# Two graph layers in seven-product form: the first product of each group is put by ScalarE into the PSUM bank in which the second accumulates

## The chip, the cores and the metric

The kernel runs on one core of a Trainium2 chip. The metric is the device time of one execution in microseconds, as the median of several runs. The engines are named as in the profile: PE is TensorE (PEld its weight loads), DVE is VectorE, ACT is ScalarE, POOL is GpSimd, SP is SyncE, which here only issues DMAs.

## The reference

There are 64 graphs of 256 nodes with 512 features; all data are float32. Layer 0 applies three graph convolutions and a residual layer norm, layer 1 a linear graph attention and again a residual layer norm:

```python
gcn(x, W, b) = einsum('bnm,bmh->bnh', adj, x @ W) + b
h = relu(gcn(x, W1, b1)); h = relu(gcn(h, W2, b2))
x = layernorm(x + gcn(h, W3, b3))
q, k = split(x @ Wqk, 2, axis=-1); v = x @ Wv
agg = einsum('bij,bjd->bid', adj, k * mask)
w = mask * einsum('bid,bid->bi', q, agg) / sqrt(512)
out = layernorm(x + softmax(w, axis=1)[:, :, None] * v)
```

## The kernel before

**Pairs and products.** Two graphs are worked on at once (a pair, `G = 2`), so there are 32 pairs. Every matrix product is cut into two by two blocks and done with seven block products in place of eight (Strassen's form). Some operands of the seven products are sums or differences of blocks, made beforehand on DVE or POOL; which of the two makes which is the list `ON_DVE` (read by `unit`, lines 61 and 62). `a_sums` makes those of the node features (tile `S`, or in place in `hT` or `xT`), `adj_sums` those of the adjacency matrix (`aS`, `aT`), `t_sums` those of the gather (`T`), and `support` those of its own output (`sup`, names ending in T5 to T7). The name's prefix tells the place: `h1` and `h2` are the outputs of the first and second aggregation, `c1` to `c3` the three supports, `x` the input features, `a` the adjacency matrix.

**A group.** `seven` (line 104) is a generator with seven steps, one product in each, in the order P1, P7, P6, P2, P5, P4, P3. It holds three PSUM banks, `x`, `v` and `y`, out of eight that are handed out in turn (`bank`). P1 is made in `x` and copied out as `t1` by `out` (ACT copies it to a `tmp` buffer in SBUF; where the group has an addend `plus`, DVE adds that instead). P6, P5 and P3 then accumulate in `x` on top of P1, P4 on top of P7 in `v`. P2 has the bank `y` alone, and the first output block is `c11(y, t1)`: a DVE addition of that bank and the SBUF copy. P6 cannot start before `out` has read P1, since both are in the same bank.

**Eleven groups for a pair.** Three `support` (the products with W1, W2, W3; line 290), two `aggregate` (adjacency times the support, line 331, followed by a relu on ACT, `relu`, line 322), one `adj_times` in `back` (the third convolution with its residual, line 367), one `adj_times` for the gather (line 367), and four in `attention` (`inner` with the letters a, b, c, d; line 546), of which `back`, c and d have an addend. The weights of `attention` come through a ring of seven DMA buffers.

**The order of work.** The schedule is written out by hand: nothing reorders instructions afterwards, and each engine works its own instructions in the order in which the program issues them. Each pass of the main loop advances several generators, letter by letter, by a string: F is `front` (supports and aggregations of pair i), S is `sums` (operand sums for pair i + 1), B is `back` of pair i - 1, G and M its gather and `attention`, E (X and Y at the end) the softmax and last norm, `finish`. `START` serves the first pass, `ORDER` the steady ones, `LAST` and `END` the last two. SP's DMA issues stand in the same order.

**In `back`**, after the layer norm statistics (`bn_stats`, line 444, `inv_std`, lines 374 to 378), `apply` writes the normalised rows: ACT makes `xm` (line 460), DVE makes `r` in place (line 462), and DVE transposes follow (line 488). The transposed rows go through DRAM (`via`, lines 492 and 494) and come back as `x1T`, from which `attention` makes `Z` (lines 524 and 527) and POOL makes `I` (line 59).

Of the kernel before, what the change touches and what calls it, by code (L numbers as in the profile page):

```python
# [9 lines left out]
FP = mybir.dt.float32  # L10
# [4 lines left out]
P = 128  # L15
PAIR = 2
G = PAIR
# [3 lines left out]
def gcn_then_graph_attention(ctx: ExitStack, tc: tile.TileContext, xT, xN, adjT, mask, W1, b1, W2, b2, W3, b3,  # L21
                             WqT, WkT, Wv, out):

    nc = tc.nc
    NPAIR = xT.shape[0]
    N, D = 256, 512
    NH, DC = N // P, D // P
    HD = D // 2
# [2 lines left out]
    KEYS = ("T1", "T2", "T3", "T4")  # L31
    SUP = 9
    SBUFS = 6
    TMP = 5
    ON_DVE = ('a5', 'c2T5', 'c2T6', 'c3T6', 'c3T7', 'h13', 'h23', 'h27', 'x3', 'x5')

    const = ctx.enter_context(tc.tile_pool(name="const", bufs=1))
    pool = ctx.enter_context(tc.tile_pool(name="work", bufs=1))
    small = ctx.enter_context(tc.tile_pool(name="small", bufs=2))
    dram = ctx.enter_context(tc.tile_pool(name="dram", bufs=2, space=bass.MemoryType.DRAM))  # L40
    psum = ctx.enter_context(tc.tile_pool(name="psum", bufs=8, space=bass.MemoryType.PSUM))

    E = mybir.EngineType
    ctx.enter_context(tc.manual_schedule(engines={E.PE, E.DVE, E.Activation, E.Pool, E.SP}))

    def bank(shape=(P, G, N)):
        return psum.tile(list(shape), FP, name="ps", tag="ps")

    def tmp():
        return pool.tile([P, D], FP, name="tmp", bufs=TMP)  # L50

    def add(o, a, b):
        nc.vector.tensor_tensor(o, a, b, op=OP.add)  # L53
# [50 lines left out]
    def seven(mm, shape, c11, c12, c21, c22, plus=None):  # L104

        def out(ps, k):
            t = shaped(shape)
            if plus is None:
                nc.scalar.copy(t, ps)  # L109
            else:  # L110
                add(t, ps, plus[k])
            return t

        x = bank(shape)
        mm(1, x, True)
        t1 = out(x, 0)
        yield
        v = bank(shape)
        mm(7, v, True)
        yield  # L120
        mm(6, x, False)
        u = out(x, 1)
        yield
        y = bank(shape)
        mm(2, y, True)
        t7 = out(v, 2)
        c11(y, t1)
        yield
        mm(5, x, False)
        c22(x, t7)  # L130
        yield
        mm(4, v, False)
        c21(v, u)
        yield
        mm(3, x, False)
        c12(x)
        yield
# [22 lines left out]
    ident = const.tile([P, P], FP, name="ident")  # L160
    make_identity(nc, ident)

    def warm(n):

        ps = bank((P, P))
        for _ in range(n):
            nc.tensor.matmul(ps, lhsT=ident, rhs=ident, start=True, stop=True)

    warm(10)
    wl = {}  # L170
    begin, end = load_w(W1, 1, True)
# [5 lines left out]
    for n, b in ((1, b1), (2, b2)):  # L177
        t = const.tile([P, DC], FP, name=f"b{n}")
# [103 lines left out]
    def support(src, w, who, last=None):  # L282

        sup = lambda: pool.tile([P, G, HD], FP, name="sup", tag="sup", bufs=SUP)
        C = {k: sup() for k in (3, 1, 5, 7, 6)}

        def mm(n, ps, first):
            for g in range(G):
                for c in range(2):
                    nc.tensor.matmul(ps[:, g], lhsT=src[n][:, c, g], rhs=w[n][:, c],  # L290
                                     start=(first and g == 0 and c == 0), stop=(g == G - 1 and c == 1),
                                     skip_group_check=True)

        def c21(v, t):
            add(C[5], v, t)
            unit(who + "T7", C[7], C[3], C[5], OP.subtract)
            unit(who + "T6", C[6], C[7], C[1])

        def c12(x):
            C[2], C[4] = sup(), sup()  # L300
            nc.scalar.copy(C[2], x)  # L301
            unit(who + "T5", C[5], C[5], C[1], OP.subtract)
            sub(C[4], x, C[6])
        steps = seven(mm, (P, G, HD), lambda y, t: add(C[3], y, t), c12, c21, lambda v, t: add(C[1], v, t))
        for _ in range(2):
            next(steps)
            yield
        if last is not None:
            last()
        yield from steps  # L310
        return C

    def aggregate(C, aS, b, who):

        hT = [pool.tile([P, 2, G, N], FP, name="hT", tag="act", bufs=2) for _ in range(2)]
        src, first, rest, last = a_sums(blocks(hT), who)
        blk = blocks(hT)

        def relu(i, j, ps=None):
            o = blk(i, j)  # L320
            for c in range(2):
                nc.scalar.activation(o[:, c], (o if ps is None else ps)[:, c], AF.Relu, bias=b[:, 2 - 2 * j + c:3 - 2 * j + c])  # L322

        def block(i, j, a, t):
            add(blk(i, j), a, t)
            relu(i, j)

        def mm(n, ps, first):
            for c in range(2):
                for g in range(G):  # L330
                    nc.tensor.matmul(ps[:, c, g], lhsT=C[n][:, g, c * P:(c + 1) * P], rhs=aS[n][:, g],  # L331
                                     start=(first and c == 0 and g == 0), stop=(c == 1 and g == G - 1),
                                     skip_group_check=True)
        for k, _ in enumerate(seven(mm, (P, 2, G, P), lambda y, t: block(0, 0, y, t), lambda x: relu(0, 1, x),
                                    lambda v, t: block(1, 0, v, t), lambda v, t: block(1, 1, v, t))):
            if k == 5:
                first()
            if k == 6:
                rest()
            yield  # L340
        return src, last
# [21 lines left out]
    def adj_times(aS, mov, c11, c12, c21, c22, plus=None):  # L363

        def mm(n, ps, first):
            for g in range(G):
                nc.tensor.matmul(ps[:, g], lhsT=aS[n][:, g], rhs=mov[n][:, g], start=(first and g == 0),
                                 stop=(g == G - 1), skip_group_check=True)
        yield from seven(mm, (P, G, HD), c11, c12, c21, c22, plus=plus)
# [63 lines left out]
    def back(i, C, aS, x, mask_t, end, put):  # L433
        r = pool.tile([P, G, NH, D], FP, name="r", tag="xT" if end else "r", bufs=1)
        xb = lambda h, j: x[:, :, h, j * HD:(j + 1) * HD]
        rb = lambda h, j: r[:, :, h, j * HD:(j + 1) * HD]
# [3 lines left out]
        def block(o, a, b, h=None):  # L440
            add(o, a, b)
            if h is not None:
                for g in range(G):
                    nc.vector.bn_stats(st[:, h, g], r[:, g, h, :])
                for g in range(G):
                    nc.vector.bn_aggr(mvt[:, h, g], st[:, h, g])
        yield from adj_times(aS, C, lambda y, t: add(rb(0, 1), y, t), lambda x: block(rb(0, 0), x, xb(0, 0), 0),
                             lambda v, t: block(rb(1, 1), v, t, 1), lambda v, t: add(rb(1, 0), v, t),
                             plus=(xb(0, 1), xb(1, 1), xb(1, 0)))

# [49 lines left out]
        gb = lambda h, j: gt[:, h, :, j * HD:(j + 1) * HD]  # L500

        def gather():
            steps = adj_times(aS, xS, lambda y, t: add(gb(0, 0), y, t), lambda x: nc.scalar.copy(gb(0, 1), x),
                              lambda v, t: add(gb(1, 0), v, t), lambda v, t: add(gb(1, 1), v, t))
            for n, _ in enumerate(steps):
                if n == 6:
                    put["gt"] = gt
                    if i + 2 < NPAIR:
                        aTs[i + 2] = load_adj(i + 2)
                yield  # L510
# [4 lines left out]
    def attention(i, x1b, w, r, mask_t, put):  # L515
# [23 lines left out]
        def inner(q, R, more=None):  # L539

            outer = OUTER[q]

            def mm(n, ps, first):
                wt = ring.pop(at[0])
                for k, o in enumerate(outer):
                    nc.tensor.matmul(ps[:, k], lhsT=left[n](place[o]), rhs=wt[:, k], start=(first and k == 0),  # L546
                                     stop=(k == len(outer) - 1), skip_group_check=True)
                fetch(at[0] + RING)
                at[0] += 1
            if more is None:  # L550
                c12, plus = lambda x: nc.scalar.copy(R[:, :, 0, 1], x), None
            else:
                c12 = lambda x: add(R[:, :, 0, 1], x, more[:, :, 0, 1])
                plus = (more[:, :, 0, 0], more[:, :, 1, 0], more[:, :, 1, 1])
            return seven(mm, (P, len(outer), HD), lambda y, t: add(R[:, :, 0, 0], y, t), c12,
                         lambda v, t: add(R[:, :, 1, 0], v, t), lambda v, t: add(R[:, :, 1, 1], v, t), plus=plus)
        v = pool.tile([P, G, NH, D], FP, name="v", tag="v", bufs=1)
        flat = lambda R: R.rearrange("p g j f -> p g (j f)")
# [35 lines left out]
    def finish(i, prev, gs=range(G)):  # L594
# [22 lines left out]
        for k, g in enumerate(gs):  # L617
            for h in range(NH):
# [2 lines left out]
                yield  # L621
            nc.sync.dma_start(out[i, :, g * NH * D:(g + 1) * NH * D].rearrange("p (h f) -> p h f", h=NH), v[:, g])

    ORDER = ("BBFEFFBEBFBFBFBFFFBEFFFFBFSFBBBFFFBBBFGFFGGFFGFEEGMFFGMMMEGMMSFFMEMMEMMEFESMMEEFFMSM"
             "SMMMFMMMMFFEMMMMMMMMSMMMMMMFSMMMSSMMSSM")
    START = ("FFFBFBBFFBFBBBBBFFFFFFBBBBBFBBBBBBBBBBBFFBBBBSBFFBSBFBBFFFBBFBBFBFSFBFFBBBBFBBSFFBSB"
             "BSFBSFFSBBBSBBBBBSFBBBBBSBSBB")
    LAST = ("FBBSEFBFEBBFFBFBFBFFBFFFFEBBFFBBFBFBEFEEGFEGGFFEGEFFMMGSFFGMMMMFEFMMMMEMMMMMMEMMMFMM"
            "GSMMMMEMMMMMMMMFMMMSSMMMFMSSSFMFFSFSFSM")
    END = ("BEBBBBBBEBBBBBBBBGMGMEMMBEGGEEMGEGEMMMMMMEMEEMEMMMMMMMMMMMGMMBMMMMMMMMMMXMMXXMMMXYXM"  # L630
           "XMYXYMYYMYXYMYXYBMYMMXXYYXM")

    def run(order, rest, **gens):
        res = {}
# [81 lines left out]
```

## Time and profile before

| What | Value |
|---|---|
| time, median of 3 runs | 2762.32 us (2762.25 to 2767.2) |
| the profiled execution's own time | 2765.32 us |
| its span, first to last instruction | 2763.5 us |
| granted TensorE clock in it | 0.996 |
| PE busy | 2716.9 us, 98% |
| PEld busy | 2401.7 us, 87% |
| DVE busy | 2145.0 us, 78% |
| ACT busy | 1133.1 us, 41% |
| POOL busy | 1262.8 us, 46% |
| DMA engines busy, mean | 46.9% |

The float32 matmul of the program is recorded as two MATMUL rows with two LDWEIGHTS rows; counts of rows are therefore twice the counts of instructions. A MATMUL row's duration overlaps the next row's, so the pace of PE is read from start to start, not from the durations. A wait is listed as "engine line waited for": who sat idle, and who ended it.

### The profile page before, as it was taken

How to read it: one execution, taken by the hardware profiler on the slowest of the kernel's cores; microseconds unless marked ns; L12 is line 12 of the kernel's file. 1: busy time of each engine (PE TensorE's matmuls, PEld its weight loads, DVE VectorE, ACT ScalarE, POOL GpSimd, SP SyncE). 2: the span in 40 equal slices, each digit the busy share in tenths (PEclk: the TensorE clock that was granted, in tenths of full speed). 3: DMA queues.
4: the chain of work that ended last, by engine and by line, in shares of the span. 5: the costliest groups of instructions: out<-in, count | busy, mean ns of one | idle time of the engine just before them, and what ended most of it. 6: DMA issues, size and time to landing. Idle time of an engine off the chain costs nothing. (4 is left out here: it accounts for less than half of the span.)

```text
span 2763.5 us, 41007 instructions
## 1 busy us (share of the span) xinstructions
PE 2716.9 (98%) x14290; PEld 2401.7 (87%) x14290; DVE 2145.0 (78%) x3828; ACT 1133.1 (41%) x2050; POOL 1262.8 (46%) x966
## 2 busy tenths in 40 slices
PE   9999999999999999999999999999999999999996
PEld 8888888888888888888888888888888888888885
DVE  5778777877777777778777777877787877778777
ACT  3434344434344343443334443434433444434343
POOL 3535455444554354544445543445544455434442
PEclk9999999999999999999999999999999999999998
DMA  6534554344544445543455444455434554434553
GB/s 209 165 110 147 165 175 135 117 143 154 163 151 123 126 147 162 173 135 112 143 162 162 141 129 131 147 162 176 133 115 141 161 162 148 130 123 147 162 155 97
DMA packets 202233, 403.71 MB, mean 146 GB/s; under 512 B 24752, under 2 KB 61872, under 8 KB 193968
## 3 DMA queue, kind: packets, MB, share of 16 engines
q1 hardware_dynamic: 202032, 401.10, 46.5%
q8 instruction: 117, 1.92, 0.3%
q14 instruction: 84, 0.69, 0.1%
HBM read 328.54 MB, written 72.48 MB: 145 GB/s over the span
## 5 line engine op out<-in xcount | busy, mean ns | idle before, releaser
L109 ACT COPY tmp<-ps 128x512 f32<-128x512 f32 x768 | 431.3, 584 | 643.3 <-PE ps L290 257.1
L62 POOL TENSOR_TENSOR sup<-sup 128x512 f32<-128x512 f32 x160 | 218.1, 1372 | 565.9 <-DVE sup L53 409.2
L546 PE MATMUL ps<-ring,I 128*128 128x256 f32 x1792 | 433.0, 381 | 7.7 <-DVE tmp L53 3.0
L546 PEld LDWEIGHTS ps<-ring,I 128*128 128x128 f32 x1792 | 334.1, 190 | 66.3 <-DVE R L53 11.7
L290 PE MATMUL ps<-w_T,S 128*128 128x256 f32 x1536 | 351.0, 381 | 9.2 <-POOL S L62 7.6
L301 ACT COPY sup<-ps 128x512 f32<-128x512 f32 x96 | 56.2, 586 | 722.2 <-PE ps L290 722.2
L290 PEld LDWEIGHTS ps<-w_T,S 128*128 128x128 f32 x1536 | 286.7, 190 | 59.7 <-POOL S L62 20.5
L546 PE MATMUL ps<-ring,Z 128*128 128x256 f32 x1344 | 327.9, 380 | 1.1 <-ACT Z L524 1.1
L59 POOL TENSOR_TENSOR I<-Z 128x384 f32<-128x384 f32 (+1 forms) x128 | 190.1, 1504 | 244.5 <-DVE Z L527 150.8
L546 PEld LDWEIGHTS ps<-ring,Z 128*128 128x128 f32 x1344 | 254.4, 190 | 38.4 <-ACT Z L524 3.3
L331 PEld LDWEIGHTS ps<-aT,sup 128*128 128x128 f32 x2048 | 253.5, 192 | 13.2 <-issue 6.6
L331 PE MATMUL ps<-aT,sup 128*128 128x128 f32 x2048 | 261.8, 276 | 1.8
L53 DVE TENSOR_TENSOR R<-ps,tmp 128x512 f32<-128x512 f32 (+1 forms) x384 | 221.2, 616 | 48.7 <-PE ps L546 48.4
L62 POOL TENSOR_TENSOR x<-x,b3b 128x512 f32<-128x512 f32 x128 | 192.2, 1523 | 128.7 <-DMA x<-in_xN 119.3
L290 PE MATMUL ps<-w,hT 128*128 128x256 f32 x1024 | 242.0, 379 | 0.0
L290 PE MATMUL ps<-w_T,hT 128*128 128x256 f32 x1024 | 236.5, 379 | 0.0
L290 PEld LDWEIGHTS ps<-w_T,hT 128*128 128x128 f32 x1024 | 194.6, 190 | 26.5
L53 DVE TENSOR_TENSOR sup<-ps,tmp 128x512 f32<-128x512 f32 x288 | 192.8, 677 | 30.8 <-PE ps L290 30.7
L290 PEld LDWEIGHTS ps<-w,hT 128*128 128x128 f32 x1024 | 192.0, 190 | 24.7
L331 PE MATMUL ps<-aS,sup 128*128 128x128 f32 x1536 | 206.3, 279 | 1.7 <-ACT tmp L109 1.1
L322 ACT ACTIVATE hT<-hT,b 128x256 f32<-128x256 f32 x384 | 167.4, 501 | 87.1 <-DVE hT L53 86.2
L331 PEld LDWEIGHTS ps<-aS,sup 128*128 128x128 f32 x1536 | 188.9, 192 | 11.4 <-DVE hT L53 4.8
(116 smaller groups left out, 4762.8 us busy)
## 6 DMA issues: line engine op xcount, KB each, us to landing
ring<-mv SPq DMA_DIRECT2D x672, 256.0 KB, 3.6
x<-in_xN SPq DMA_DIRECT2D x32, 1024.0 KB, 8.0
out<-v SPq DMA_DIRECT2D x64, 512.0 KB, 7.6
xT<-in_xT SPq DMA_DIRECT2D x31, 1024.0 KB, 5.0
via<-tr SPq DMA_DIRECT2D x31, 1024.0 KB, 4.2
x1T<-via SPq DMA_DIRECT2D x124, 256.0 KB, 4.7
ring<-mv SPq DMA_DIRECT2D x224, 128.0 KB, 3.1
aT<-in_adjT SPq DMA_DIRECT2D x32, 512.0 KB, 3.9
```

The source lines that it names most:

```text
L53: nc.vector.tensor_tensor(o, a, b, op=OP.add)
L59: (nc.gpsimd).tensor_tensor(o, a, b, op=op)
L62: (nc.vector if name in ON_DVE else nc.gpsimd).tensor_tensor(o, a, b, op=op)
L109: nc.scalar.copy(t, ps)
L290: nc.tensor.matmul(ps[:, g], lhsT=src[n][:, c, g], rhs=w[n][:, c], start=(first and g == 0 and c == 0), stop=(g == G - 1 and c == 1), skip ...
L301: nc.scalar.copy(C[2], x)
L322: nc.scalar.activation(o[:, c], (o if ps is None else ps)[:, c], AF.Relu, bias=b[:, 2 - 2 * j + c:3 - 2 * j + c])
L331: nc.tensor.matmul(ps[:, c, g], lhsT=C[n][:, g, c * P:(c + 1) * P], rhs=aS[n][:, g], start=(first and c == 0 and g == 0), stop=(c == 1 and ...
L546: nc.tensor.matmul(ps[:, k], lhsT=left[n](place[o]), rhs=wt[:, k], start=(first and k == 0), stop=(k == len(outer) - 1), skip_group_check= ...
```

## The change

A group gets its bank `y` from a tag of its own with two banks (`seed_bank`); the eight banks become six and two. Once P1 is in `x`, ACT copies it into `y`, a copy from PSUM to PSUM (with an addend, DVE adds it on the way). P2 is then issued without the start flag, so that it accumulates on top of P1 in `y`. The callback `c11` gets the finished block: it is an ACT copy or, in `aggregate`, the relu straight from PSUM, where before it was a DVE addition. Two banks are first written by matmuls, eight in all, at the start of the program. The list `ON_DVE` is another one: new on it are a3, a6, a7, c1T6, c1T7, c2T7, h17, h25 and h26; c2T5, c3T6 and h13 have left it, to POOL. The four order strings are other ones.

```diff
     TMP = 5
-    ON_DVE = ('a5', 'c2T5', 'c2T6', 'c3T6', 'c3T7', 'h13', 'h23', 'h27', 'x3', 'x5')
+    SEEDS = 2
+    ON_DVE = ('a3', 'a5', 'a6', 'a7', 'c1T6', 'c1T7', 'c2T6', 'c2T7', 'c3T7', 'h17', 'h23', 'h25', 'h26', 'h27', 'x3', 'x5')
...
-    psum = ctx.enter_context(tc.tile_pool(name="psum", bufs=8, space=bass.MemoryType.PSUM))
+    psum = ctx.enter_context(tc.tile_pool(name="psum", bufs=8 - SEEDS, space=bass.MemoryType.PSUM))
...
+    def seed_bank(shape=(P, G, N)):
+        return psum.tile(list(shape), FP, name="seed", tag="seed", bufs=SEEDS)
...
         x = bank(shape)
         mm(1, x, True)
-        t1 = out(x, 0)
+        y = seed_bank(shape)
+        if plus is None:
+            nc.scalar.copy(y, x)
+        else:
+            add(y, x, plus[0])
         yield
...
-        y = bank(shape)
-        mm(2, y, True)
+        mm(2, y, False)
         t7 = out(v, 2)
-        c11(y, t1)
+        c11(y)
...
+    seeds = [seed_bank((P, 4, P)) for _ in range(SEEDS)]
+    for t in seeds:
+        for k in range(4):
+            nc.tensor.matmul(t[:, k], lhsT=ident, rhs=ident, start=(k == 0), stop=(k == 3), skip_group_check=True)
     warm(10)
...
-        steps = seven(mm, (P, G, HD), lambda y, t: add(C[3], y, t), c12, c21, lambda v, t: add(C[1], v, t))
+        steps = seven(mm, (P, G, HD), lambda y: nc.scalar.copy(C[3], y), c12, c21, lambda v, t: add(C[1], v, t))
...
-        for k, _ in enumerate(seven(mm, (P, 2, G, P), lambda y, t: block(0, 0, y, t), lambda x: relu(0, 1, x),
+        for k, _ in enumerate(seven(mm, (P, 2, G, P), lambda y: relu(0, 0, y), lambda x: relu(0, 1, x),
...
-            return seven(mm, (P, len(outer), HD), lambda y, t: add(R[:, :, 0, 0], y, t), c12,
+            return seven(mm, (P, len(outer), HD), lambda y: nc.scalar.copy(R[:, :, 0, 0], y), c12,
...
-    ORDER = ("BBFEFFBEBFBFBFBFFFBEFFFFBFSFBBBFFFBBBFGFFGGFFGFEEGMFFGMMMEGMMSFFMEMMEMMEFESMMEEFFMSM"
-             "SMMMFMMMMFFEMMMMMMMMSMMMMMMFSMMMSSMMSSM")
+    ORDER = ("BBFEFFBEFBBFBFBFFBFFFFFBBBFBBBFFGSFFFGEGFGGFFGEFMMGMEMFEFMFMEMFMMEMFMSMFMSEMSEESMMF"
+             "SSMFFMMMSEMMFSFMMMMMMMMSMMMMMEMMMMMSMMF")
...
```

The two `adj_times` calls change as the `inner` line does; `START`, `LAST` and `END` change as `ORDER` does.

More of the change, by code (lines that the diff above doesn't have):

```diff
@@ L446, in block @@
                     nc.vector.bn_aggr(mvt[:, h, g], st[:, h, g])
-        yield from adj_times(aS, C, lambda y, t: add(rb(0, 1), y, t), lambda x: block(rb(0, 0), x, xb(0, 0), 0),
+        yield from adj_times(aS, C, lambda y: nc.scalar.copy(rb(0, 1), y), lambda x: block(rb(0, 0), x, xb(0, 0), 0),
                              lambda v, t: block(rb(1, 1), v, t, 1), lambda v, t: add(rb(1, 0), v, t),
@@ L502, in gather @@
         def gather():
-            steps = adj_times(aS, xS, lambda y, t: add(gb(0, 0), y, t), lambda x: nc.scalar.copy(gb(0, 1), x),
+            steps = adj_times(aS, xS, lambda y: nc.scalar.copy(gb(0, 0), y), lambda x: nc.scalar.copy(gb(0, 1), x),
                               lambda v, t: add(gb(1, 0), v, t), lambda v, t: add(gb(1, 1), v, t))
@@ L622, in finish @@
             nc.sync.dma_start(out[i, :, g * NH * D:(g + 1) * NH * D].rearrange("p (h f) -> p h f", h=NH), v[:, g])
-    ORDER = ("BBFEFFBEBFBFBFBFFFBEFFFFBFSFBBBFFFBBBFGFFGGFFGFEEGMFFGMMMEGMMSFFMEMMEMMEFESMMEEFFMSM"
-             "SMMMFMMMMFFEMMMMMMMMSMMMMMMFSMMMSSMMSSM")
[L626 to L631, printed above, removed]
+    ORDER = ("BBFEFFBBEFBBFBFBFFBFFFFFBBBFBBBFFGSFFFGEGFGGFFGEFMMGMEMFEFMFMEMFMMEMFMSMFMSEMSEESMMF"
+             "SSMFFMMMSEMMFSFMMMMMMMMSMMMMMEMMMMMSMMF")
+    START = ("BBBFFFFFBFFBBBBBFFFFFFFBBBBFBBBFBSBBBBBBSBBBBBBFBFSBFBBFFBFBFFFBBBBFBFBBBFBFBSFFBBBS"
+             "BBSFSBBBBFBBBFBSBBSBSSFSBBBBB")
+    LAST = ("FFBEFBBBEBBFFBFBFFBFFFFSFBSFFFBBBFBBFFEGEFEGGFGFFGMMGFMFGMEMFFMEMMMMMMMMMFFMMEMEEFEF"
+            "MSFSMFEMSSMMMFMMSMMMMMMSMMMMESFMMMMSSMM")
+    END = ("BBEBBBBBEBBBBBBBBGBGMEGEGMEMEMMGMEEGMMMEMMEMMMEEMMMMMGMMMBMMMMBMMMMMMMMMMXMMXMXMMXYX"
+           "MMXYYMXXYYXYYMXYYXYYMMYXMMM")
     def run(order, rest, **gens):
```

## The prediction, made before the changed kernel was run

> **What bounds the kernel now.** First the page: the busy times and the slices.
>
> ```profile
> PE 2716.9 (98%) x14290; PEld 2401.7 (87%) x14290; DVE 2145.0 (78%) x3828; ACT 1133.1 (41%) x2050; POOL 1262.8 (46%) x966
> ...
> PE   9999999999999999999999999999999999999996
> PEclk9999999999999999999999999999999999999998
> ```
>
> PE is busy in every slice at the full clock, except in the last. Busy is not yet at its pace, so I turned to the timeline. In the stretch 1096:1122, eight MATMUL rows of 256 columns start at 1098.33 and the next row at 1100.06: 0.216 us a row. Eight of 128 columns start at 1107.83, the next at 1108.72: 0.112. The groups by shape hold 10,304 rows of 256 columns and 3,712 of 128, some 270 small ones besides: 10,304 x 0.216 + 3,712 x 0.112 + about 31 = 2,672 us. The first matmul starts at 1.4, the last ends 9.3 before the span's end. So of 2763.5 about **80 to 84 us** are gaps between matmuls: 8 in the first 86 us, 21 in the last 100, and in between (by start-to-start distance above the pace) 1.2 to 2.8 in each stretch of 86, about **1.75 us for a pair**. That is all that the other four engines can give back in the steady part; the rest is PE's own pace.
>
> Where are these gaps? The waits of PE and PEld name two kinds that can be traced to one place each:
>
> ```profile
> PEld ps L290 <- POOL S L62: 20.5, 32, 0.8
> PEld ps L546 <- DVE R L53: 12.4, 30, 0.9
> PE ps L290 <- POOL S L62: 7.6, 32, 0.4
> PEld ps L546 <- DVE tmp L53: 7.1, 11, 1.0
> ```
>
> (us in total, times, longest.) The first comes once for each pair, and the timeline shows it with the end of the first aggregation:
>
> ```profile
> 1111.76 1.86 PEld L331 LDWEIGHTS ps<-aT,sup 128*128 128x128 f32 x16 [0.22 <-issue]
> 1112.10 0.67 DVE L53 TENSOR_TENSOR hT<-ps,tmp 128x512 f32<-128x512 f32 x1
> 1112.87 2.62 ACT L322 ACTIVATE hT<-hT,b 128x256 f32<-128x256 f32 x6 [0.74 <-DVE hT L53]
> 1113.02 1.52 DVE L53 TENSOR_TENSOR hT<-ps,tmp 128x512 f32<-128x512 f32 x2 [0.25 <-PE ps L331]
> 1113.77 1.16 PE L331 MATMUL ps<-aS,sup 128*128 128x128 f32 x8
> 1114.77 1.89 PE L290 MATMUL ps<-w,hT 128*128 128x256 f32 x8
> 1115.56 1.27 POOL L62 TENSOR_TENSOR S<-hT 128x512 f32<-128x512 f32 x1 [5.11 <-ACT hT L322]
> 1116.89 3.72 PE L290 MATMUL ps<-w_T,S 128*128 128x256 f32 x16 [0.23 <-POOL S L62]
> ```
>
> P1 of the second support (1114.77, eight rows) would be over at 1116.50; P7 starts at 1116.89, when POOL has made h17. That is **0.39 us**, and it recurs: 31 times, 12.3 us in all. The other gaps of this stretch are a P5 that waits for ACT's copy of P6 (0.22), starts after a wait (0.07 to 0.12 each) and a P3 that waits for DVE (0.12). The second kind lies in the c and d products of line 546, where P5 and P3 wait for DVE's copy or sum of the same bank: up to 0.77 us in one pair, none in another, about 11 us in all.
>
> **What the Trainium skill says.** "PSUM — Partial Sum Buffer", The four PSUM rules: writes by ScalarE or VectorE leave the has_written bits alone, and a matmul without the first flag adds to what an engine has written where the bit is set. That is what the eight first matmuls are for, so the change can do what it says; the trace of before holds no such write. "Perfetto Trace Analysis", Optimizing Scalar/DVE Operations: a ScalarE operation has about 51 ns of access overhead on PSUM and 93 on SBUF. The trace has no copy into PSUM; the nearest row is ACT tmp<-ps, 584 ns. The same section says that GpSimd and DVE share an SBUF port. The trace agrees: S<-hT on DVE (h27) takes 984 ns where POOL works beside it, S<-hT,S 671; sums of POOL go from 1.27 to 1.5 us.
>
> **The change part by part.** The order of the built program, engine by engine, was laid beside before's.
>
> 1. *DVE and ACT.* Each group loses one DVE addition: 352, of which 320 at 0.68 and 32 at 0.415 us by their rows, 231 us of 2145. ACT gains a copy in nine of eleven groups (288; 256 at 0.585 and 32 of half the size): about 160 us. The SBUF copy of P1 becomes the PSUM copy, and the relu reads PSUM in place of SBUF (463 for 501 ns). Neither engine is the bound, so this by itself is worth **0**; its cover is PE, with 98%.
>
> 2. *The new dependence.* P2 waits for the copy into y. But P6 comes before P2 in each group and always waited for the same reading of P1, since it accumulates in that bank. In the built order no P2 waits for a copy. So the chain P1, copy, P6 is the one to price. In the first aggregation P6 follows P1 by one product of 0.90 us; the copy starts 0.2 after P1 and takes 0.58, and about 0.1 goes to the start: 0.88. Before, the same place cost 0.09 and 0.07. By the nearest row: **0**. Bounds: 0.04 less by the skill's overheads, which gives at most 1 us over 31 pairs; 0.2 more, if copies within PSUM were slower, some 6 us loss. In all other groups P6 starts 1.7 us or more after P1, which covers even that.
>
> 3. *Banks.* Two for y, six for x and v. A third group's copy waits for the c11 of the group two earlier; ACT and the program have it in that order anyway, and P2 of that group is long issued. Six banks that turn in twos come round after three groups, eight that turn in threes after 2.67. **0**; cover: the order itself, in which each bank's last reader stands well over 1 us before the next start.
>
> 4. *h17 to DVE.* POOL was idle for 5.1 us before it, so no queue held it; its own 1.27 us did. On DVE, with POOL idle beside it, 0.68: the chain is 0.6 shorter, the gap was 0.39. It stands in DVE's order right behind the addition that feeds the relu, and DVE waits there for ACT (0.9 us) with nothing urgent behind it but row transposes. **-0.39 x 31 = -12 us**. Bounds: 0 (if relu is later by what item 6 says) and -15 (with the slow start of P6 behind it).
>
> 5. *c and d.* DVE loses both c11 additions that stood in its order between the sums for P5 and P3. In the new order P5's sum is done 0.7 us before PE comes to it, and P3's 0.85 (by rows of 0.6 and 0.41 us from start to start); in the old one P3 had 0.25. **-10 us** of the 11, bounds 0 and -13. The ring of SP is the new limit there: the new order has up to 20 M steps with no F between them, 14 before. Landing is 3.6 us median, seven buffers ahead are at least 4.3; three waits of 0.5 to 0.7 were seen. Up to +5 us.
>
> 6. *The apply on ACT.* In the new order the first `apply` (0.80 us; 0.74 from start to start) stands before the copies of P6 and P7 of the first aggregation; before, it came after four relus. It waits for DVE's norm scale. DVE works without a pause for 11 us before: four v updates of 0.66, three additions to r, four statistics of 0.6, five sums of sup, and the small ones of the scale among them. Added up from the softmax column, the scale is there 0.5 us before P6 ends, so the copy is late by 0.2 and P5 by 0.2, about the 0.22 that P5 already waits. **0**, bounds -3 and +30 (below).
>
> 7. *Other units.* a3, a6, a7, c1T6, c1T7, c2T7, h25, h26 go to DVE, c2T5, c3T6, h13 to POOL: with h17 192 more on DVE net. By the rows (three of 0.42, six of 0.7, less three of 0.7) that is 107 us, which leaves DVE some 124 below before; POOL loses about 210 (rows of 0.7 to 1.4). c1T6 and c1T7 feed the first aggregation's P6 and P7; DVE has them 0.2 to 0.6 us before. h13 is ready 1.4 us before its P3. **0**, for the cover of item 5's DVE slack; bounds +-5.
>
> 8. *SP.* 1,275 DMAs as before, and the via store stands between the same ring loads. The last transpose ends where it did (0.2 us apart by the same sums), so Z comes when it came. **0**, +-2.
>
> 9. *Start and end.* Eight cold matmuls: 16 rows at 0.223 (warm(10) takes 4.46 us for 20) = 3.6 us, of which P7's 1.74 and P6's 0.39 us of waiting for weights and S take up 2.1: **+1.5**. The end keeps its chain of scores, softmax and norm: 0, +-2.
>
> Sum: -12 - 10 + 1.5 = -20.5. Because items 4 to 7 all stand on slacks under a microsecond, of which some will be used up, I take 2.5 back: **-18 us**. Against the profiled execution, 2765.3 (span 2763.5 and 1.8 around it), that is 2747.3; the median of the runs shown is 3.0 below that execution, so 2744.3, put at **2744**.
>
> **Rivals.** *(A) Small gain*, as above: 2728 to 2756, chance 0.64. *(B) Nothing*: P7's gap turns into waits of P5 and P3 behind the apply, and c and d are held by the ring: -12 - 10 + 1.5 + 31 x 0.65 = 0, 2762, within 0.2%. For it speaks that the timeline has five short gaps one behind another there; against it, that DVE loses work. Chance 0.14. *(C) Slower*: DVE's 16 longer operations before the scale take their full rows, not their distances: 16 x 0.08 = 1.3 us later. Then P7 of the first aggregation waits for c1T7 and P5 behind the apply, together 1.2 more in each pair: +37, less 10 of c and d and item 4's gain lost, +1.5: +28, 2790. It decides from where the scale is over 0.8 us later than summed. The rows measured back to back in the old stretch speak against it. Chance 0.22. That the bank would not accumulate is excluded by the eight matmuls; it would not change the time.
>
> **Numbers.** Range 2730 to 2774: A and B whole, and C's nearer part. A measurement of this kernel tells about 0.2%, 5.5 us, from no change. Faster 0.64, within 0.14, slower 0.22. A's own range is 2728 to 2756.
>
> **What would show it.** PE's rows and pace the same, gaps down to about 1.1 us for a pair; L290's wait for S at P7 gone, L546's waits for DVE under 3 us; DVE near 2020, ACT near 1300, POOL near 1050. Wrong if PE waits for ACT at line 342 (the aggregation's line in the changed kernel) by over 0.5 us in each pair, or for the ring.

## The result and the profile after

The changed kernel takes **2786.79 us** (median of 6 runs, 2783.62 to 2788.93) against 2764.03 for the kernel before (6 runs beside it): a ratio of **1.008, 95% interval 1.0067 to 1.0093**. It is 23 us slower; 18 us faster was forecast, with a range of 2730 to 2774. The profiled execution took 2786.89 us, with a span of 2785.1 at a granted clock of 0.995.

(In the diff under "The change" one letter is missing: the new `ORDER` begins `BBFEFFBBEFBBFBFBFFBFFFFFBBBF`.)

The page after, the same rows as before:

```profile
PE 2711.8 (97%) x14306; PEld 2410.4 (87%) x14306; DVE 2146.5 (77%) x3668; ACT 1276.8 (46%) x2338; POOL 1102.6 (40%) x774
...
PE   9999999999999999999999999999999999999996
...
PEclk9999999999999999999999999999999999999997
```

Clock and pace are as before, PE still fills every slice. DVE has lost 160 instructions and yet is as busy as before (2020 was forecast). The waits of PE and PEld (us in total, times, longest):

```profile
PE ps L342 <- ACT tmp L113: 27.0, 31, 0.9
PE ps L557 <- ACT Z L535: 13.7, 26, 1.4
```

```profile
PEld ps L342 <- issue: 32.0, 31, 1.0
PEld ps L557 <- ACT Z L535: 27.1, 35, 1.8
```

The waits for `S` and for `R` that led the list before are gone from its head. Two others stand there, and both were priced at nothing: PE waits for ScalarE at line 342, the aggregation, once for each pair, which the prediction had named as its sign of error; and PE waits for Z.

The timeline at the end of the first aggregation shows the first (start, us, engine, line, operation):

```profile
1116.98 1.68 POOL L66 TENSOR_TENSOR sup<-sup 128x512 f32<-128x512 f32 x1 [23.26 <-DVE sup L66]
...
1117.39 0.57 ACT L122 COPY seed<-ps 128x512 f32<-128x512 f32 x1 [0.36 <-PE ps L342]
1117.65 1.02 DVE L389 SCALAR_TENSOR_TENSOR nb<-mvt,rs 128x4 f32<-128x4 f32 x1
1118.61 0.68 DVE L60 TENSOR_TENSOR sup<-ps,sup 128x512 f32<-128x512 f32 x1
...
1119.01 1.06 PE L342 MATMUL seed<-aT,sup 128*128 128x128 f32 x8
...
1119.27 0.15 DVE L467 SCALAR_TENSOR_TENSOR mnb<-nb,mask 128x4 f32<-128x4 f32 x1
1119.51 0.81 ACT L471 ACTIVATE xm<-r,mnb,mrs 128x512 f32<-128x512 f32 x1 [1.55 <-DVE mnb L467]
1120.23 1.05 ACT L113 COPY tmp<-ps 128x512 f32<-128x512 f32 x2
...
1120.93 1.24 PE L342 MATMUL ps<-aT,sup 128*128 128x128 f32 x9 [0.87 <-ACT tmp L113]
```

Read it from the bottom. P5 (1120.93) waits for ScalarE's copy of P6. P6 was issued to its last row when P2 began, at 1119.01, so the copy could have run 0.2 us later; it starts at 1120.23, because the first `apply` stands in front of it on ScalarE. That `apply` waited for the scale, `mnb`. And the scale is late by one operation: `nb`, four elements in each of 128 partitions, takes **1.02** us. In the kernel before it took 0.16:

```profile
1111.42 0.16 DVE L378 SCALAR_TENSOR_TENSOR nb<-mvt,rs 128x4 f32<-128x4 f32 x1
```

POOL's sum c1T5 runs from 1116.98 to 1118.66, and `nb` ends when it ends. That is so in 31 pairs: each time `nb` ends 0.02 us after the sum.

To see where the time went I sorted PE's gaps (start to start, less the pace of 0.216 and 0.112 us) by the product that was late, for every profiled kernel. "Ends" are the first 86 and the last 110 us; the other columns are the 30 odd pairs between. P7 is that of the second support, which needs h17; P6 is the next product there; P5 that of the first aggregation (all its gaps between aT products); I are the products of line 557 with sums of Z.

| kernel | time | P7 | P6 | P5 | Z | I | P3s and other | ends | all gaps |
|---|---|---|---|---|---|---|---|---|---|
| before | 2764.0 | 12.3 | 3.2 | 9.0 | 2.1 | 13.7 | 13.2 | 30.1 | 83.6 |
| changed | 2786.8 | 0.0 | 0.0 | 34.3 | 22.6 | 5.3 | 10.1 | 31.2 | 103.5 |
| seeding, old order | 2806.0 | 12.1 | 3.2 | 9.0 | 1.0 | 53.7 | 13.0 | 28.1 | 120.1 |
| before + h17 on DVE | 2784.3 | 0.0 | 13.7 | 9.0 | 4.5 | 10.3 | 35.0 | 27.4 | 100.1 |
| before, seven banks | 2801.5 | 12.2 | 3.2 | 9.0 | 1.7 | 50.6 | 13.2 | 30.7 | 120.8 |
| changed + c1T5 on DVE | 2755.4 | 0.0 | 0.0 | 24.9 | 0.0 | 3.9 | 10.3 | 28.9 | 68.0 |
| changed + early scale | 2766.2 | 0.0 | 0.0 | 17.7 | 21.1 | 4.6 | 10.0 | 31.3 | 84.6 |
| changed + both | **2732.6** | 0.0 | 0.0 | 1.4 | 0.0 | 4.6 | 10.3 | 31.9 | 48.3 |
| both, h17 on POOL | 2748.0 | 12.1 | 3.2 | 1.4 | 0.3 | 6.4 | 9.8 | 31.4 | 64.6 |

The second row less the first: P7 and P6 give 15.5 back, I 8.4, the rest 2; P5 takes 25.3 and Z 20.5. That is +19.9 of the 21.6 by which the span grew.

### The profile page after: what moved, and what is told of

It is laid out like the page before. It is cut to its first block, busy times and chain, and to the rows that moved or that the text cites. A ratio compares the mean times of both kernels' runs of the same rounds, so it can differ in the third digit from the quotient of the medians.

```text
span 2785.1 us, 41190 instructions
## 1 busy us (share of the span) xinstructions
PE 2711.8 (97%) x14306; PEld 2410.4 (87%) x14306; DVE 2146.5 (77%) x3668; ACT 1276.8 (46%) x2338; POOL 1102.6 (40%) x774
## 5 line engine op out<-in xcount | busy, mean ns | idle before, releaser
L113 ACT COPY tmp<-ps 128x512 f32<-128x512 f32 x512 | 280.2, 586 | 205.2 <-PE ps L301 114.3
L557 PE MATMUL ps<-ring,Z 128*128 128x256 f32 x896 | 226.2, 384 | 13.8 <-ACT Z L535 13.7
L57 DVE TENSOR_TENSOR sup<-ps,tmp 128x512 f32<-128x512 f32 x192 | 130.5, 680 | 136.3 <-PE ps L301 136.3
L342 PEld LDWEIGHTS ps<-aT,sup 128*128 128x128 f32 x1536 | 193.7, 192 | 38.4 <-issue 32.0
L342 PE MATMUL ps<-aT,sup 128*128 128x128 f32 x1536 | 199.5, 277 | 27.0 <-ACT tmp L113 27.0
L122 ACT COPY seed<-ps 128x512 f32<-128x512 f32 x256 | 146.8, 574 | 161.9 <-PE ps L301 120.5
L557 PEld LDWEIGHTS ps<-ring,Z 128*128 128x128 f32 x896 | 164.8, 190 | 47.4 <-ACT Z L535 27.1
L301 PE MATMUL ps<-w,S 128*128 128x256 f32 x768 | 181.6, 380 | 3.0 <-DVE sup L57 3.0
L566 ACT COPY R<-seed 128x512 f32<-128x512 f32 (+1 forms) x128 | 67.0, 549 | 242.0 <-PE seed L557 219.1
L57 DVE TENSOR_TENSOR R<-ps,tmp 128x512 f32<-128x512 f32 (+1 forms) x256 | 149.2, 617 | 25.8 <-PE ps L557 24.9
```

The costliest lines, as they stand in the source:

```text
L122: nc.scalar.copy(y, x)
L566: return seven(mm, (P, len(outer), HD), lambda y: nc.scalar.copy(R[:, :, 0, 0], y), c12, lambda v, t: add(R[:, :, 1, 0], v, t), lambda v, ...
```

## The experiments

Two explanations stood against each other at first. **Theory (port):** POOL's sum holds the small DVE operation that makes the scale, and everything behind it follows. **Rivals:** the seeding costs by itself (copies into PSUM, six banks); or DVE's order is simply too full, and `nb` is only where that shows.

### Seeding with the old order

```
 (the changed kernel, with these of the kernel before)
 ON_DVE = ('a5', 'c2T5', 'c2T6', 'c3T6', 'c3T7', 'h13', 'h23', 'h27', 'x3', 'x5')
 ORDER, START, LAST, END
```

> The seven-product groups of the changed kernel (P1 written into the bank of P2, two banks kept), with the order of steps and the units on VectorE of the kernel before. Theory (port): the loss of the change comes from the new order and not from the seeding. Without it the scale of the norm comes long before it is wanted, so P5 of the first aggregation waits no more than 0.3 us; P7 still waits 0.39 us for h17, c and d lose 4 to 10 us of their waits (fewer sums on VectorE), and the start costs 1.5: 2752 to 2762 us. Rival (seeding costs): the copies into PSUM and the two banks hold PE whatever the order: 2775 us or more, with P6 or P5 waiting for ScalarE by 0.5 us or more in each pair.

Measured: 2806.05 us, ratio 1.0151 (1.0137 to 1.0165). Both expectations failed. The time is what the rival gave, but not by its wait: P5 waits 0.22 as before, P6 no more than before. The 40 us stand at one product, the first of c and d with I, 1.4 us in each pair. The timeline there:

```profile
1147.34 3.62 POOL L63 TENSOR_TENSOR I<-Z 128x512 f32<-128x512 f32 x2 [8.39 <-DVE Z L538]
1148.88 1.03 PE L557 MATMUL ps<-ring,Z 128*128 128x256 f32 x4
1150.36 0.68 DVE L57 TENSOR_TENSOR gt<-ps,tmp 128x512 f32<-128x512 f32 x1
1151.04 1.28 POOL L63 TENSOR_TENSOR I<-I,Z 128x512 f32<-128x512 f32 x1
1151.14 1.10 PE L557 MATMUL ps<-ring,I 128*128 128x256 f32 x4 [1.23 <-POOL I L63]
```

The profile names POOL. But the first of the two I sums, the one that this product reads, ended at 1149.3, and the kernel before had the same sums at the same distance without a wait. What ends 0.1 us before the start is DVE's `gt<-ps`, at 1151.04: the sum that reads a bank of the gather. In 30 pairs the weight load of this product starts 0.070 to 0.071 us after the end of that sum, while its distance to POOL's second sum varies from 0.138 to 0.146. This points to the bank: of six, it comes round one reader too early. The next run tests that.

### Seven banks, nothing seeded

```
-psum = ... tc.tile_pool(name="psum", bufs=8, ...)
+psum = ... tc.tile_pool(name="psum", bufs=7, ...)
```

> The kernel before with seven PSUM banks in place of eight, nothing seeded. Theory (banks): in the old order of steps the banks are used to the last one; the first products of c and d of line 546 come to wait for the gather's and the aggregation's sums on VectorE, as they do in the run that seeds with the old order (where the wait is 1.4 us at c's P7): 1 to 2.5 us in each pair, 2790 to 2840. Rival (eight banks had slack, and the wait in that run is GpSimd's sum I, which the profile names): within 0.3% of before.

Measured: 2801.52 us, ratio 1.0127 (1.0112 to 1.0143), as the theory gave. The I column rises by 37, the whole of the loss, and no other moves. The old order of steps has no bank to spare. The list of waits names nobody for it ("issue"), but the timeline shows whom the first of these products waits for. Of the two sums in the first line, the one that ends first does so at 1152.85:

```profile
1152.17 1.27 DVE L53 TENSOR_TENSOR hT<-ps,tmp 128x512 f32<-128x512 f32 x2
1152.92 0.73 PEld L546 LDWEIGHTS ps<-ring,I 128*128 128x128 f32 x4 [1.02 <-issue]
```

In 30 pairs the load starts 0.07 us after the end of that `hT` sum, which reads a bank too; these waits make 24 us.

So a kernel that keeps two banks for seeds needs another order of steps, and the changed kernel's has it: its I column is 5.3. The counterpart, the new order without seeds, was not run, so what the seeding alone is worth stays open.

### h17 alone

```
-ON_DVE = (..., 'h13', 'h23', ...)        (kernel before)
+ON_DVE = (..., 'h13', 'h17', 'h23', ...)
```

> The kernel before with one edit: h17 on VectorE in place of GpSimd. Expected by the prediction's item 4: the 0.39 us that P7 waits in each pair goes, and nothing else moves: 31 x 0.39 = 12 us less, 2752 us. Rival: VectorE's sum stands in front of the additions that PE wants next (P3, P5 of the weights' product), or comes no sooner since VectorE is behind: 2760 to 2766, with a new wait for VectorE there.

Measured: 2784.32 us, ratio 1.0073 (1.006 to 1.0085); the rival's kind of loss, larger than it gave. P7's gap is gone. The timeline shows what came for it:

```profile
1121.41 0.69 DVE L62 TENSOR_TENSOR S<-hT 128x512 f32<-128x512 f32 x1 [0.97 <-ACT hT L322]
...
1122.09 0.15 DVE L456 SCALAR_TENSOR_TENSOR mnb<-nb,mask 128x4 f32<-128x4 f32 x1
...
1122.33 0.81 ACT L460 ACTIVATE xm<-r,mnb,mrs 128x512 f32<-128x512 f32 x1 [0.95 <-issue]
```

In the old order `mrs` and `mnb` stand behind h17, and h17 waits for ScalarE's last relu. The first `apply` starts 1.67 us after P1 of the second support (1120.66), before it was 0.62. P6 then waits for a copy behind the apply, and P3 of the same support for a DVE sum behind the normalized rows and their transposes: 10.5 and 21.8 us. The edit pays only where nothing that the chain needs is queued behind h17.

### c1T5 on DVE, the scale early, and both

```
 ON_DVE: + 'c1T5'                            (first)
 back:   rs, nb = inv_std(mvt)
-        yield                               (second)
         mrs = ...; mnb = ...
+        yield
```

> The changed kernel with one more unit on VectorE: c1T5 leaves GpSimd, so that no GpSimd sum runs beside the small operation nb that makes the norm's scale. Theory (port): nb falls from about 0.97 to 0.2 us; but c1T5 now takes 0.68 us of VectorE ahead of the scale, so that the scale comes only 0.1 to 0.3 us sooner and P5 still waits some 0.8 us: 2775 to 2787. Rival (VectorE's order is too full, nb is only where it shows): nb stays long or the scale comes 0.6 us later, P5 waits 1.5 us or more: 2795 to 2810.

> The changed kernel with mrs and mnb right behind nb (the half of the run with both edits that leaves c1T5 on GpSimd). Theory (port): nb is still held to about 0.97 us by GpSimd's sum, but the first apply starts some 0.55 us sooner than in the changed kernel, since one addition less stands between nb and mnb; P5's wait falls from 1.03 to some 0.5 us, Z's waits shrink by about two thirds: 2757 to 2768, between the run with c1T5 alone on VectorE and the changed kernel. Rival (only VectorE's own queue matters, GpSimd's sum does no harm): as fast as the run with both edits, 2730 to 2740, with nb at 0.2.

> The changed kernel with c1T5 on VectorE and with the two operations mrs and mnb, which make the scale, right behind the norm's nb instead of one step later. Theory (port): the scale is there 0.8 us or more sooner, the first apply ends before ScalarE's copies of P6 and P7 are due, P5's wait falls from 1.03 to 0.1 us or less, and Z comes about 1 us sooner, so that its waits (11 us) shrink too: 2745 to 2758. Rival (the seeding or the full VectorE holds PE): P5 waits, or other waits take over, 2775 or more.

Measured, with the ratio to before:

| | c1T5 on POOL | c1T5 on DVE |
|---|---|---|
| scale one step later | 2786.79, 1.008 (changed kernel) | 2755.37, 0.997 (0.9959 to 0.9982) |
| scale right behind nb | 2766.21, 1.0002 (0.9994 to 1.001) | **2732.59, 0.9886 (0.9872 to 0.9899)** |

Taking c1T5 from POOL gives 31 to 34 us, the early scale 21 to 23, and they add up. With both, in the same stretch:

```profile
1097.46 0.16 DVE L389 SCALAR_TENSOR_TENSOR nb<-mvt,rs 128x4 f32<-128x4 f32 x1
...
1097.66 0.16 DVE L466 SCALAR_TENSOR_TENSOR mnb<-nb,mask 128x4 f32<-128x4 f32 x1
1097.74 0.68 DVE L66 TENSOR_TENSOR sup<-sup 128x512 f32<-128x512 f32 x1
1097.90 0.81 ACT L471 ACTIVATE xm<-r,mnb,mrs 128x512 f32<-128x512 f32 x1
...
1099.01 1.07 ACT L113 COPY tmp<-ps 128x512 f32<-128x512 f32 x2 [0.29 <-PE ps L342]
...
1099.70 1.55 PE L342 MATMUL ps<-aT,sup 128*128 128x128 f32 x12
```

`nb` is back at 0.16, the apply is over before P6 is (P2 begins at 1098.81), and P5 follows P2 after eight rows of 0.112. DVE has 32 operations of 0.69 more here than in the changed kernel, so a DVE that is too full is ruled out. Seeding and six banks are the same in all four, and the fastest is 32 us below the kernel before, so they do not make the 23 us by themselves. The rival of the early scale, that POOL's sum does no harm, gave 2730 to 2740; it fell too, with `nb` still at 1.02 and P5's wait at 0.50.

Two details of the expectations failed: the early scale was to shrink Z's waits by two thirds and left 21.1 of 22.6, and c1T5 on DVE came 20 us below its range, all of it at Z. (Both edits together came 12 us below theirs.) So Z isn't late because of the scale. It has a hold of its own. Of the four normalizing operations of a pair (`r<-r,rs,nb`, line 473) the second stands behind h17 in DVE's order, whenever the scale was there. In the changed kernel:

```profile
1125.37 1.62 DVE L473 TENSOR_SCALAR r<-r,rs,nb 128x512 f32<-128x512 f32 x1
1125.43 1.27 POOL L66 TENSOR_TENSOR S<-hT,S 128x512 f32<-128x512 f32 x1 [6.77 <-DVE S L66]
```

and with c1T5 on DVE:

```profile
1109.49 0.55 DVE L473 TENSOR_SCALAR r<-r,rs,nb 128x512 f32<-128x512 f32 x1
1109.62 1.56 POOL L66 TENSOR_TENSOR S<-hT,S 128x512 f32<-128x512 f32 x1 [32.27 <-DVE S L66]
```

POOL's h16 starts 0.06 us behind the operation in one and is let through first; in the other it starts 0.13 us behind and is the one that waits. From P1 of the second support (medians over 24 pairs) the last transpose ends and the first copy of Z ends:

| kernel | last transpose | first copy of Z | PE at its first Z |
|---|---|---|---|
| before | 8.94 | 21.17 | 22.23 |
| changed | 7.02 | 19.74 | 19.92 |
| changed + early scale | 7.02 | 19.81 | 19.92 |
| changed + c1T5 on DVE | 5.96 | 19.12 | 19.92 |
| both | 5.96 | 19.12 | 19.92 |

The hold moves the end of the transposes by 1.06 us, the early scale by nothing. It isn't new: in the kernel before the same operation took 1.64 us in 30 pairs. But the slack of 1.06 us that Z had there (22.23 less 21.17) is 0.18 in the changed kernel. Why POOL's start shifts by 0.07 us isn't settled; it had stood idle for 32.27 us there, against 6.77.

The medians hide something. Z's waits aren't spread evenly: 17.8 of the 22.6 us stand in 10 of 30 pairs. In just these ten the store of the transposed rows, `via`, landed 5.6 to 6.2 us after its issue, in the other twenty after 4.2 to 4.3. And in each of the ten a DMA of 16 KB from another queue (q8, which the page lists as "instruction") began 0.9 to 2.2 us after the issue of the store, in none of the twenty. Of the stretches 1044.9:1051.2 (first two lines) and 1130.9:1137.2 (the third):

```profile
q8 instruction: 1, 0.02, 1.7%
via<-tr SPq DMA_DIRECT2D x1, 1024.0 KB, 6.1
...
via<-tr SPq DMA_DIRECT2D x1, 1024.0 KB, 4.3
```

With the early scale it is the same (11 pairs, 17.1 of 21.1 us). In the two kernels with c1T5 on DVE such a DMA comes 3.9 us after the issue at the earliest, and the store never takes over 4.8. So c1T5 on DVE brings two things at once: the transposes end 1.06 us sooner, and no q8 transfer begins early in the store. Which of them frees Z the runs don't separate; the second was planned by nobody, and is luck. That the small DMA delays the store is read from the coincidence, not tested.

### The apply behind the copies

```
-ORDER = "BBFEFFBBEFBBFBFBFFBFFFFFBBBF...
+ORDER = "BBFEFFBBEFBBFBFBFFFFFBFFBBBF...     (changed kernel)
```

> The changed kernel with the step that holds the first apply put behind P6, P2 and the copies of P6 and P7 of the first aggregation in the order string (two steps of the front between). Theory: P5's wait of 1.03 us at the first aggregation goes (to 0.1 or less), which proves that the apply in front of the copies made it; but the apply itself starts later beside PE's work by 1.5 us or so, and Z, which had no slack left, is late by as much more: its waits grow from 22 to 50 us or more, so that the time is 2790 to 2815. Rival (the apply's place alone costs, Z has slack): 2752 to 2760.

Measured: 2820.35 us, ratio 1.0194 (1.018 to 1.0208). P5's gap falls to the level of small starts (4.4 for all pairs), so the apply in front of the copies did make it. But the loss isn't at Z (15.1, less than in the changed kernel); it is at P3 of the same aggregation, whose gap grows by 61 us:

```profile
1137.10 0.83 ACT L471 ACTIVATE xm<-r,mnb,mrs 128x512 f32<-128x512 f32 x1
1137.96 0.55 DVE L473 TENSOR_SCALAR r<-r,rs,nb 128x512 f32<-128x512 f32 x1 [2.33 <-ACT xm L471]
1138.55 1.03 DVE L499 STREAM_TRANSPOSE tr<-r 128x256 f32<-128x256 f32 x2
1139.44 1.25 DVE L57 TENSOR_TENSOR hT<-ps,tmp 128x512 f32<-128x512 f32 x2
1140.15 1.05 PE L342 MATMUL ps<-aS,sup 128*128 128x128 f32 x7 [1.99 <-DVE hT L57]
```

The step moves DVE's part too. DVE stands idle for 2.33 us before the normalizing operation, and the sum `hT`, which PE needs for P3, waits behind it. That chain was in no expectation; a step moved for ScalarE's sake moves every engine's queue. Another 10 us come from PE itself: behind the wait, in 7 pairs, some rows of 256 columns start 0.427 us apart instead of 0.216. The next run shows more of that.

### h16 on DVE

```
 ON_DVE: + 'h16'                              (changed kernel)
```

> The changed kernel with one more unit on VectorE: h16, the sum that GpSimd begins 0.06 us after VectorE's second normalizing operation (r<-r,rs,nb, line 473) and during which that operation takes 1.62 in place of 0.55 us. Theory (Z is late in part for this): the second operation falls to 0.55, h16 itself takes 0.68 of VectorE ahead of it, so that the last transpose ends some 0.4 us sooner; Z's waits fall from 22 to about 10 us, P5's wait stays at 1.03: 2772 to 2780. Rival (Z is late only since the scale is late, the held operation has slack): 2785 or more, up to 2806 with 0.68 more on VectorE.

Measured: 2926.2 us, ratio 1.0582 (1.0567 to 1.0596), far from both. h16 doesn't stand ahead of the held operation in DVE's order; between h17 and h16 stand three normalizing operations and six transposes:

```profile
1179.45 1.62 DVE L473 TENSOR_SCALAR r<-r,rs,nb 128x512 f32<-128x512 f32 x1
1179.52 1.27 POOL L66 TENSOR_TENSOR hT<-hT 128x512 f32<-128x512 f32 x1 [6.78 <-DVE S L66]
...
1184.83 0.66 DVE L66 TENSOR_TENSOR S<-hT,S 128x512 f32<-128x512 f32 x1
...
1185.64 3.44 PE L301 MATMUL ps<-w_T,S 128*128 128x256 f32 x8 [3.15 <-DVE S L66]
1188.91 1.89 PE L301 MATMUL seed<-w,hT 128*128 128x256 f32 x8
```

PE waits 3.15 us for it, and then its eight rows take 3.44 us where the next eight take 1.89. In the stretch right behind the wait the granted clock, the third number from the right, is 0.50:

```profile
1185.60:1188.00 2.40, 2.36 (x6) 1.94 (x7) 0.48 (x1) 0.00 (x0) 1.76 (x2) 0.50 0.89 333
```

It is so in 29 of 30 pairs, for 5 to 13 rows. Of the 139 us over the changed kernel the waits make 99 and the rows at half the pace 48; Z's 22 go, since PE comes later. And the operation is held as before: POOL's next sum has taken h16's place beside it. So this run doesn't test what it was meant to.

### h17 back on POOL

```
 ON_DVE: - 'h17'                              (the kernel with both edits)
```

> The kernel with both edits (c1T5 on VectorE, mrs and mnb early), but with h17 back on GpSimd, which undoes the prediction's item 4 where nothing else holds PE. Theory: P7 of the second support waits again for GpSimd's h17, 0.39 us in each pair, and h16 behind it comes later: 2742 to 2750, against 2732.6. Rival (in the new order GpSimd's h17 comes in time): 2730 to 2735.

Measured: 2748.04 us, ratio 0.9944 (0.993 to 0.9957), inside the theory's range. The gap of 0.39 is back at P7 (12.1) and the slow start at P6 behind it (3.2): 15.3 together, and the times differ by 15.5.

```profile
PEld ps L301 <- POOL S L66: 20.3, 32, 0.8
```

### The port by itself

```
for f in forms:              # one form of DVE operation at a time
    8 x nc.gpsimd.tensor_tensor(c, a, b, op=add)     # 128x512, in SBUF
    10 x f()                 # e.g. scalar_tensor_tensor(n, s, -1.0, u), 128x4
```

> VectorE's operations by themselves, ten of each form one behind another, first beside eight sums of GpSimd (128x512, all in SBUF), then with GpSimd idle; none of the reference is computed. Theory (port): small operations with two SBUF sources (the form of nb, and an addition of 128x4) take 0.15 us with GpSimd idle and wait for the end of a running GpSimd sum beside it, so that one of them takes about as long as a GpSimd sum (1 us or more); those with one SBUF source, or one of PSUM and one of SBUF, are not held (0.15 to 0.2). Rival: nb was long for another reason, all small forms keep 0.15 to 0.3 us beside GpSimd.

Measured, minimum, median and maximum in ns over both halves. (Sums of POOL ran beside parts of the second half too, so what counts is whether a sum ran beside the operation.)

```profile
L47 DVE SCALAR_TENSOR_TENSOR n<-s,u x20: 161/232/1251, 3.0 to 27.0; 128x4 f32<-128x4 f32 x20
L49 DVE TENSOR_SCALAR n<-s x20: 164/170/1252, 13.7 to 36.3; 128x4 f32<-128x4 f32 x20
L50 DVE RECIPROCAL n<-s x20: 178/178/178, 15.8 to 38.4; 128x4 f32<-128x4 f32 x20
L51 DVE SCALAR_TENSOR_TENSOR n<-q,u x20: 149/155/161, 17.9 to 107.6; 128x4 f32<-128x4 f32 x20
L53 DVE TENSOR_TENSOR o<-q,b x20: 682/691/693, 83.4 to 127.5; 128x512 f32<-128x512 f32 x20
```

Line 47 is the form of `nb`. One by one it takes 0.16 when it falls between two POOL sums and 1.11 when a sum has begun; it ends 0.02 us after the sum. An addition of 128x512 with two SBUF sources takes 1.63 beside the sums and 0.69 without them. With one source in PSUM (`q`, lines 51 and 53) it is never held, at 128x4 or at 128x512. The reciprocal isn't held either. The theory had one thing wrong: `tensor_scalar`, with a single SBUF source, is held like the others, which is why `r<-r,rs,nb` was.

The Trainium skill says this: "SBUF — State Buffer", SBUF: two separate sides, calls the pair of ports that DVE and GpSimd share an exclusive lock; whoever starts first has it for the whole instruction, and on DVE's side operations with two SBUF inputs or in a mode that uses two ports ask for it. These runs agree, and add what it means for small ones: 0.16 us becomes 1.1. One reading has to be made with care: by the recorded starts POOL's h16 came 0.06 us behind the normalizing operation and yet went first, so within a tenth of a microsecond the recorded order doesn't tell who has the ports.

## Why the prediction was wrong

- **Bound and pace: right.** PE's pace is unchanged in the changed kernel, and the times follow the gaps: 48.3 us of gaps at 2732.6, 103.5 at 2786.8. Only behind the waits of over 2 us in the runs with the later apply and with h16 on DVE do rows come at half the pace.
- **Items 1 and 2 (copies, new dependence): right where they can be seen.** The seed copy takes 574 ns (x256), the SBUF copy 586. P6 of the first aggregation starts 0.09 us behind its neighbour, as before.
- **Item 3 (banks): right for the new order (I column 5.3), by its cover and not by its count.** The cover was the order itself, in which each bank's last reader stands well ahead. The count (round after three groups instead of 2.67) would have said the same of the old order, and there six banks cost 40 us at one product, and seven without seeds 37.
- **Item 4 (h17): right.** -12 was taken, -15 was its bound; the kernel with both edits, with h17 on DVE and on POOL, measures -15.5. The condition that it named, nothing urgent behind h17 on DVE, is the one that fails in the old order.
- **Item 5 (c and d): right.** -10 forecast, -8.4 in the steady part; the ring wasn't waited for.
- **Item 6 (the apply): the first of two steps that failed.** Its place and its direction were named with a bound of +30; its value was 0, and it measured +25.3. The sum over DVE's operations had the scale half a microsecond before the end of P6. One term was off: "the small ones of the scale" were taken at their rows of before, and `nb`, 0.16 there, took 1.02. In the timeline the scale is there at 1119.42 and P6 ended at about 1119.0, so of the 0.9 us by which the sum missed, the hold is 0.86. The prediction itself cited that GpSimd and DVE share a port, and used it for the long rows alone. In the kernel before no POOL sum stood beside `nb`; the change left c1T5 on POOL, and the new order puts it there.
- **Item 8 (Z): the second step that failed.** 0 +-2 was forecast, +20.5 measured. "Z comes when it came" looked at the transposes alone, and didn't ask when PE wants Z: against P1 of the second support they end 1.9 us sooner than before, but PE comes 2.3 us sooner, so that a slack of 1.06 us was down to 0.18. And it took the store behind them at its time of before: in 10 of 30 pairs it lands 1.3 to 2.0 us later, and there stand 17.8 of Z's 22.6 us. The transposes would have ended 1.06 us sooner but for the hold of the second `r<-r,rs,nb`. With c1T5 on DVE both the hold and the late stores are gone and the Z column is 0.0; how much each is worth stays open.
- **DVE's load (item 7): wrong.** 2146 instead of 2020. The rows that were to take 0.16 to 0.7 take more beside POOL: `nb` 52.7 us for 10.4 (with those of the last norm, 0.68 each), and sums on DVE up to twice their rows (`S<-hT,S` 1.01 us for 0.67, `hT<-hT` 1.51). As item 1 said, DVE's sum of busy times isn't the bound; one hold on the chain was.
- **Start and end (item 9):** the first product of W1 starts 1.5 us later than before (7.45 for 5.92), but its P2 0.3 sooner (13.34 for 13.65), so the waits there took up more than the eight matmuls cost. The gaps of both ends together grew by 1.1.
- **The rivals.** C gave 2790 and named P5 behind the apply. That the number came close is luck: its late scale was put down to 16 longer operations at 0.08 each, its P7 does not wait, and Z's 20 us aren't in it. The condition that it stated, a scale over 0.8 us later than summed, is what came about.

## What to carry to other kernels

When a sum moves between engines, look up what will then run beside each small operation on the chain, not only beside the long ones: an operation of 0.16 us that shares a port with one of 1.3 us can take 1.1, and whatever is queued in order behind its result pays again. Where such an operation stands on a chain with under a microsecond of slack, move the neighbour away and issue the chain's small operations back to back before trusting any sum of rows. And an order of steps is fitted to its banks and its units together: each of the edits here (six banks, seven banks, h17, h16, a later apply) cost 20 to 140 us in an order that was not made for it, and the version with two small repairs is 32 us faster than the kernel before. Last, a median over pairs hides a loss that a third of them carry: look at a wait pair by pair before naming its cause.

## What the runs showed of the hardware

A DVE operation of 128x4 with two SBUF sources, or a `tensor_scalar` with one, ended with the POOL sum that had started first (1.11 us for 0.16); an addition of 128x512 with two SBUF sources took 1.63 for 0.69, and a copy of 128x512 from SBUF to SBUF 1.37 for 0.43. A reciprocal of 128x4 (0.178) and the two forms tried with one source in PSUM (0.15 at 128x4, 0.69 at 128x512) kept their times. A POOL sum whose recorded start lies 0.06 to 0.09 us behind that of the normalizing operation went first, one 0.13 us behind waited. After a wait of 3.15 us PE's next rows came at half the pace, with a granted clock of 0.50. In the changed kernel a store of 1 MB landed after 5.6 to 6.2 us instead of 4.2 to 4.3 in the ten pairs in which a 16 KB DMA of queue q8 began early in it. And the releaser that the profile names for a wait on several events can be the wrong one: POOL's I for DVE's `gt`.
